# Attention outputs turned by VectorE and DMA, other step counts in the layer chain, and rectified pieces moved in the projections

## The chip, the core and the metric

The kernel runs on one core of a Trainium2 chip. The metric is device time in microseconds (us), the median of the runs shown. A core has five engines with queues of their own: TensorE (PE, matrix products into PSUM), VectorE (DVE), ScalarE (ACT), GpSimd (POOL), and SyncE (SP), which here only issues DMAs.[...]

## What is computed

Four images of 256 channels and 64 x 64 pixels go through four layers, each on a group-normed input and with its result added to the image:

```
_gn(v):    group norm, 32 groups, no affine part
layer 0:   xs = relu(group_norm(conv3x3(x)));  g, theta, phi = three 1x1 convolutions of xs to 128 channels
           y = softmax(theta^T phi) g            (4096 x 4096 for each image)
           group_norm(conv1x1(y, w_w)) * 0.1 + xs
layer 1:   rms norm, q, k, v in 4 heads of 32; linear attention (q softmax over the head, k over the pixels);
           1x1 convolution, rms norm
layer 2:   depthwise 3x3 and pointwise kernels generated from the pooled image, applied to it
layer 3:   1x1 convolution with a mix of 4 experts, weights from the pooled image
x = x + layer_i(_gn(x))     for i = 0, 1, 2, 3
```

Everything is float32. The sizes that count below: N = 4096 pixels, P = 128 partitions, NH = 2 halves of the 256 channels.

## The kernel before

**Stages.** The non-local attention of layer 0 holds most of the work. Image b's attention (`attend`) runs beside what other images need at that time: the rest of image b - 1 (`tail`: the end of layer 0 in `nonlocal_out`, then `linear_attention`, `generated`, `mixed`) and the convolution of image b + 1 (`convolve`). So there is a first convolution and projection, then stages b = 0, 1, 2, each an attention and after it the projection of the next image (`project`), then stage 3 with the attention of the last image, and an end in which that image's tail is alone. Stage 0 has only the convolution of image 1 beside it; stages 1 and 2 have a tail and a convolution; stage 3 has the tail of image 2.

**Attention.** One image has NQ = 8 blocks q of 512 queries and NM = 16 steps m of 256 keys for each. A step computes `logits` (two products of phi and theta to two banks `pf`, exponentials on ACT to `pr`) one step ahead, then the products of the probabilities with g into `py`. A block is either "across" (queries on the partitions: the row sums come out as a 129th column, L1218) or not (L1221, sums added up on DVE in `tot`). Across are q = 7 of all images and, in images 1 and 2, q in TURNED = (0, 1, 3, 5, 6).

An across block is finished by `ended`. It is a generator: its first part runs in the block's last step and normalises `py` to `yn` (query rows). Then, a step of the next block for each `yield`: `yn` is turned by four PE transposes to `ps_yt` and copied by ACT to `yt` (L1183, L1188); `yt` is multiplied by `ww_s` and copied to `wt` (L1193, L1197); `projected` takes statistics of `wt` on DVE (L1122) and stores it to `wy_d`.

**The chain.** The other layers are generators, too. They yield numbers n, in units of an attention step, or None. `Chain.steps` adds n times the stage's rate to a credit, and yields one step for each whole unit; after every step `run` issues one attention step. None is one step always, and adds rate - 1 to the credit. In `convolve` of images 2 and 3 the yields are 0, and the DVE time of what is issued is owed as time / 4.35 us, without the rate. `w.later(k, f)` calls f after k steps. If the chain still has steps when the attention has none left, they are issued back to back, with only the last parts of `ended` (q = 7) between. `while next(attention, False)` then issues what is left of the attention's steps, and `run(project(), attention)` the projection, chunk by chunk, with one more attention call after each.

**Around the changed lines.** In `linear_attention`, the tail of images 0 to 2 turns each chunk of 512 pixels by DVE's 32 x 32 block transpose (`corners`), stores to DRAM that move the blocks (`sent`), and a load (`fetched`, into quarters of `ra` and `rt`); `lengths` (L1405, ACT) is the first reader. The result `z` goes the same way at the layer's end (`z_corners`, `z_sent`, `z_fetched`), and `z_added` (L1697) adds it to the image with statistics. `generated` then starts with the group norm, whose first PE instruction is `pm` (L413). At the end of `convolve`, `normed_relu` norms the result, and `piece` applies the relu to 1024 columns of a half (four activations, L805; one, L810, for image 0) and adds it to `xs_d` by DMA. Two of the eight pieces are issued in the chain; the other six wait in `relus`, and `project` issues one for each of its first six chunks of 512 columns. A chunk is four products for phi and theta (L1029) with two ACT copies (L1030), and eight for g (L1034) with a DVE addition (L1036).

Loads and stores go through SP's queue: filters for the convolution (L587), the stores and loads named above, results. The tag k2 has four buffers of 2 KB in each partition: `yn`, `yt`, and small tiles of the layers.

Of the kernel before, what the change touches and what calls it, by code (L numbers as in the profile page):

```python
# [8 lines left out]
F32 = mybir.dt.float32  # L9
# [95 lines left out]
def conv_preact_fast(ctx: ExitStack, tc: tile.TileContext, guard, in_range, x, wc, wtpg, ww, wqkv, wout, w1cat, wd2,  # L105
# [19 lines left out]
    def k2(name):  # L125
        return wk.tile([P, 512], F32, tag="k2", name=name, bufs=4)
# [893 lines left out]
    def project(first=False):  # L1020

        if first:
            nc.gpsimd.memset(g[:, :, P:P + 1], 1.0)
        for c in range(N // 512):
            cols = bass.ts(c, 512)
            for k in (1, 0):
                ps = bank("ps_tp")
                for h in range(NH):
                    nc.tensor.matmul(ps, wtpg_s[:, h, k, :], big[:, h, cols], start=(h == 0), stop=(h == NH - 1))  # L1029
                nc.scalar.activation(tpg[:, k, cols], ps, AF.Identity, bias=btp_s[:, k:k + 1])  # L1030
            ps = bank("ps_g").rearrange("p (j o) -> p j o", o=P)
            for j in range(4):
                for h in range(NH):
                    nc.tensor.matmul(ps[:, j, :], big[:, h, bass.ts(4 * c + j, P)], wtpg_s[:, h, 2, :],  # L1034
                                     start=(h == 0), stop=(h == NH - 1))
            tt(g[:, bass.ts(c, 4), 0:P], ps, bg_s.unsqueeze(1).to_broadcast([P, 4, P]), ALU.add)  # L1036
            if relus:
                relus.pop(0)()
            yield

    NM = N // CH * 4
# [1 line left out]
    wy_stats = {}  # L1043
    sum_d = tc.dram_tile([B * NQ, P, 512], F32, name="sum_d")
    rec_d = tc.dram_tile([B * NQ, 512], F32, name="rec_d")


    res_st = cp.tile([P, NH, NQ, 6], F32, name="res_st")
# [23 lines left out]
    def attend(b):  # L1072
# [93 lines left out]
        def ended(q, py, xc):  # L1166

            at = b * NQ + q
            total, r = (sp.tile([P, 4], F32, name=name) for name in ("total", "r_q"))
            for i in range(2):  # L1170
                nc.vector.tensor_copy(total[:, bass.ts(i, 2)], py[i][:, :, P])
            nc.vector.reciprocal(r, total)
            yn = k2("yn")
            tt(yn[:, 0:2 * P].rearrange("p (t o) -> p t o", o=P), py[0][:, :, 0:P],
               r[:, 0:2].unsqueeze(2).to_broadcast([P, 2, P]), ALU.mult)
            for t in range(2, 4):
                nc.scalar.activation(yn[:, bass.ts(t, P)], py[1][:, t - 2, 0:P], AF.Copy, scale=r[:, t:t + 1])
            for side, t in enumerate((total, r)):
                nc.vector.tensor_reduce(guard[:, side, at:at + 1], t, AX.X, ALU.add)
            yield  # L1180
            pt, yt = bank("ps_yt"), k2("yt")
            for t in range(4):
                nc.tensor.transpose(pt[:, bass.ts(t, P)], yn[:, bass.ts(t, P)], ident)  # L1183
            if at == B * NQ - 1:
                nc.vector.tensor_copy(yt[:, 0:2 * P], pt[:, 0:2 * P])
                nc.scalar.copy(yt[:, 2 * P:4 * P], pt[:, 2 * P:4 * P])
            else:
                nc.scalar.copy(yt, pt)  # L1188
            yield
            wt = k4("wt").rearrange("p (h n) -> p h n", h=NH)  # L1190
            for h in range(NH):
                ps = bank("ps_wy")
                nc.tensor.matmul(ps, ww_s[:, bass.ts(h, P)], yt, start=True, stop=True)  # L1193
                if at == B * NQ - 1 and h == 0:
                    nc.vector.tensor_copy(wt[:, h, :], ps)
                else:
                    nc.scalar.copy(wt[:, h, :], ps)  # L1197
            yield
            projected(q, wt, xc)
# [156 lines left out]
    def linear_attention(w, b, big, qT, k4, st, sh, sums):  # L1356
# [129 lines left out]
        if alone:  # L1486
            w.fill(1)
            warm(3)
            w.settle()
            xg, first = normed(0), ()  # L1490
            rinv, banks = turned(xg)
            first = [product(xg, j) for j in range(2)]
            next(sums)
            xt = tokens(rinv, banks)
            yield 1
            last = None
            for c in range(NC):
                if c + 1 < NC:
                    ahead = normed(c + 1)
                next(sums, None)  # L1500
                if c == 2:
                    checks.append(counted())
                if c in (2, 4, 5):
                    next(checks[0])
                yield 0.5
                this = (yield from qk_of(xg, rinv, first)), xt
                first = ()
                if c + 1 < NC:
                    xg = ahead
                    rinv, banks = turned(xg)  # L1510
                if last is not None:
                    context(c - 1, *last)
                if c + 1 < NC:
                    xt = tokens(rinv, banks)
                last = this
            yield 1
            context(NC - 1, *last)
        else:
            w.settle()
            nc.gpsimd.memset(quarters[3].rearrange("p (k o) -> p k o", k=16)[:, :, NH * 32:TW // 4], 1.0)  # L1520
            xgs = {0: normed(0)}
            s = corners(xgs[0])
            yield 0.5
            sent(0, s)
            xgs[1] = normed(1)
            s = corners(xgs[1])
            yield 0.5
            xs = {0: fetched(0)}
            sent(1, s)
            yield 1  # L1530
            rinv = lengths(xs[0])
            last, turn = None, None
            for c in range(NC):
                if c + 1 < NC:
                    xs[c + 1] = fetched(c + 1)
                if c + 2 < NC:
                    xgs[c + 2] = normed(c + 2)
                    s = corners(xgs[c + 2])
                unit(xs[c], rinv)
                yield 0.5  # L1540
                if c + 2 < NC:
                    sent(c + 2, s)
                if c % 2 == 0:
                    if c > 0:
                        q_sent(c // 2 - 1, turn)
                    turn = k4("q_turn")
                elif c > 1:
                    q_fetched(c // 2 - 1)
                qk = yield from qk_of(xgs.pop(c), rinv)
                q_corners(c, qk, turn)  # L1550
                if last is not None:
                    context(c - 1, *last)
                if c + 1 < NC:
                    rinv = lengths(xs[c + 1])
                last = qk, xs.pop(c)
            yield 0.3
            q_sent(NC // 2 - 1, turn)
            yield 0.7
            q_fetched(NC // 2 - 1)
            context(NC - 1, *last)  # L1560
# [157 lines left out]
        yield 0.7  # L1718
        zts[NC - 1] = z_fetched(NC - 1)
        z_added(NC - 2, zts.pop(NC - 2))  # L1720
        yield 1.6
        z_added(NC - 1, zts.pop(NC - 1))
        if b + 2 < B:
            nc.gpsimd.memset(ra[:, :, :, 0:1], 0.0)
# [547 lines left out]
    def run(*steps):  # L2272

        for _ in steps[0]:
            for s in steps[1:]:
                next(s, None)
# [12 lines left out]
    with tc.manual_schedule(engines={E.PE, E.Activation, E.DVE, E.Pool, E.SP}):  # L2289
        run(Chain(convolve_first).steps())  # L2290
        run(project(first=True))
        for b in range(B - 1):
            attention = attend(b)
            parts = [tail(b - 1, big, qT), lambda w: convolve(w, b + 1, 0.53)] if b > 0 else [
                scale_weights, filters_across, lambda w: convolve(w, 1, 0.87)]
            if b == 0:
                load_x(1)
            run(Chain(both(*parts), 1.365 if b == 0 else 0.785).steps(), attention)
            while next(attention, False):
                pass  # L2300
            run(project(), attention)

        held = []
        spare = [t.rearrange("p h y x -> p h (y x)")[:, h, 0:CH] for t in (ra, rt) for h in range(NH)]
        diag = tpg[:, NH, 0:9 * P].rearrange("p (k q) -> p k q", k=9), tpg[:, NH, :]
        attention = attend(B - 1)
        run(Chain(tail(B - 2, big, qT, held=held), 1.14).steps(), attention)
        end = Chain(tail(B - 1, tpg[:, 0:NH, :], tpg[:, NH, :], in_turns(spare, k4), diag, x_cols), held=held)
        last = end.steps()
        while next(attention, False):  # L2310
            pass
        next(last)
        for part, _ in enumerate(attention):
            if part == 0:
                residual_centred()
                warm(2)
            else:
                end.fill(1)
        run(last)
        assert not held and not end.unsettled  # L2320
# [572 lines left out]
```

## Time and profile before

| what | us |
|---|---|
| median of 3 runs (lowest, highest) | 2955.13 (2953.87, 2955.23) |
| the profiled execution | 2954.07 |
| its span, first to last instruction | 2952.2 |
| attention of stage 1: first logits to last product | 743.8 to 1402.6 |
| attention of stage 2 | 1456.5 to 2116.0 |
| attention of stage 3 starts | some 2170 |

The largest groups of PE, each product counted as two passes:

| line | operation | busy us |
|---|---|---|
| L1105 | logits, 128 x 512, x2048 | 972.4 |
| L1221 | products with g, not across, x1152 | 543.5 |
| L1218 | products with g, across, x3584 | 436.8 |
| L706 | convolution, x864 | 195.8 |
| L1029 | projections of phi and theta, x256 | 117.7 |
| L1193 | products with `ww_s`, across, x56 | 29.9 |
| L1183 | transposes of `yn`, x56 | 8.6 |

The mean granted clock of PE is 0.996. A line of the order of time gives start, duration, engine, line, operation, out<-in, shape and count, and in brackets the idle time of the engine just before it with the instruction that ended it. Matmuls overlap, so the pitch of successive starts tells more than the duration. A line of windows gives, for each engine, busy time and instructions in that stretch.

### The profile page before, as it was taken

The numbers are of one execution on the slowest core, as the hardware profiler recorded it, in microseconds if no ns is written. First come the engines' busy times: TensorE is split into PE (matmuls) and PEld (weight loads), VectorE is DVE, ScalarE is ACT, GpSimd is POOL, SyncE is SP. The second block draws the span as 40 slices with busy tenths as digits, with TensorE's granted clock in tenths as the row PEclk, the third lists the DMA queues.
The fourth block names the chain that finished last, engine by engine and source line by source line (L and its number), as shares of the span: only waits on it lengthen the run. The fifth ranks groups of instructions, "written<-read, shape, count | busy, mean of one in ns | idle before, by whom it ended". The sixth has DMA issues, their size and how long they took to land. (4 is left out here: it accounts for less than half of the span.)

```text
span 2952.2 us, 31046 instructions
## 1 busy us (share of the span) xinstructions
PE 2878.1 (97%) x11158; PEld 1730.1 (59%) x11158; DVE 1851.7 (63%) x2939; ACT 1345.7 (46%) x2720; POOL 182.8 (6%) x218
## 2 busy tenths in 40 slices
PE   7999999999999999999999999999999999999999
PEld 3454555556675555777577464577655544446744
DVE  8737767752446874776254696577446578873585
ACT  2234333345556544324565543422555554433774
POOL 0000000001011000000101000000000110000143
PEclk9999999999999999999999999999999999999999
DMA  6245444324444423110554342421245563235112
GB/s 229 73 88 121 69 62 75 47 33 104 127 135 139 82 86 75 54 59 31 133 155 122 97 75 86 91 67 50 70 120 123 111 125 54 25 43 132 44 68 77
DMA packets 420642, 262.70 MB, mean 89 GB/s; under 512 B 310464, under 2 KB 357312, under 8 KB 416960
## 3 DMA queue, kind: packets, MB, share of 16 engines
q1 hardware_dynamic: 120672, 239.14, 25.1%
q10 hardware_dynamic: 295200, 4.72, 8.3%
q0 software_dynamic: 4608, 16.78, 3.6%
q8 instruction: 90, 1.47, 0.2%
q14 instruction: 72, 0.59, 0.1%
HBM read 162.84 MB, written 114.53 MB: 94 GB/s over the span
## 5 line engine op out<-in xcount | busy, mean ns | idle before, releaser
L1106 ACT ACTIVATE pr<-pf 128x512 f32<-128x512 f32 x1024 | 600.4, 596 | 912.1 <-PE pf L1105 871.0
L1105 PE MATMUL pf<-tpg 128*128 128x512 f32 x2048 | 972.4, 598 | 2.4 <-ACT pr L1106 2.4
L1105 PEld LDWEIGHTS pf<-tpg 128*128 128x128 f32 x2048 | 378.4, 191 | 372.4 <-issue 348.7
L1221 PE MATMUL py<-pr,tpg 128*128 128x512 f32 x1152 | 543.5, 594 | 0.3 <-ACT pr L1106 0.3
L1218 PEld LDWEIGHTS py<-tpg,pr 128*128 128x128 f32 x3584 | 434.7, 192 | 109.5 <-issue 100.3
L1218 PE MATMUL py<-tpg,pr 128*128 128x129 f32 x3584 | 436.8, 275 | 2.6 <-ACT pr L1106 2.6
L138 DVE TENSOR_TENSOR tot<-tot,pr 128x1024 f32<-128x1024 f32 x252 | 307.5, 1220 | 165.2 <-ACT pr L1106 164.4
L1221 PEld LDWEIGHTS py<-pr,tpg 128*128 128x128 f32 x1152 | 220.3, 191 | 278.7 <-issue 269.2
L141 DVE SCALAR_TENSOR_TENSOR dw<-xp,dk,dw 128x1008 f32<-128x1008 f32 x192 | 243.1, 1270 | 7.3 <-ACT dw L1866 3.6
L706 PE MATMUL ps_conv<-v,u 128*128 128x256 f32 x864 | 195.8, 380 | 1.3 <-DVE v L138 1.1
L706 PEld LDWEIGHTS ps_conv<-v,u 128*128 128x128 f32 x864 | 161.8, 190 | 31.3 <-issue 8.8
L233 POOL TENSOR_TENSOR rstd<-rstd,half 128x2 f32<-128x2 f32 x24 | 17.7, 736 | 1941.5 <-DVE rstd L431 1795.6
L1029 PE MATMUL ps_tp<-big,wtpg_s 128*128 128x512 f32 x256 | 117.7, 597 | 6.0 <-ACT big L805 5.3
L1455 PE MATMUL ps_qk<-wqkv_s,xg 128*128 128x256 f32 x496 | 115.0, 382 | 7.1 <-ACT pr L1106 7.1
L138 DVE TENSOR_TENSOR tpg<-ps_g,bg_s 128x512 f32<-128x512 f32 x32 | 22.1, 692 | 154.5 <-PE ps_g L1034 154.5
L141 DVE SCALAR_TENSOR_TENSOR sums<-ps_conv,sums 128x512 f32<-128x512 f32 x72 | 49.7, 691 | 94.6 <-PE ps_conv L706 86.4
L1455 PEld LDWEIGHTS ps_qk<-wqkv_s,xg 128*128 128x128 f32 x496 | 93.7, 191 | 24.5 <-ACT pr L1106 7.9
L1874 PE MATMUL ps_pw<-dw,pk 128*128 128x512 f32 x192 | 86.3, 593 | 0.0
L1029 PEld LDWEIGHTS ps_tp<-big,wtpg_s 128*128 128x128 f32 x256 | 46.0, 192 | 57.5 <-issue 42.7
L1030 ACT ACTIVATE tpg<-ps_tp,btp_s 128x512 f32<-128x512 f32 x64 | 44.0, 687 | 71.7 <-PE ps_tp L1029 71.7
L1122 DVE BATCH_NORM_STATS2 wy_st<-wt 128x6 f32<-128x512 f32 x64 | 42.8, 688 | 47.8 <-ACT wt L1159 33.7
L2196 ACT ACTIVATE res<-ps_ex,b 128x512 f32<-128x512 f32 x56 | 38.2, 686 | 72.6 <-PE ps_ex L2188 69.4
(486 smaller groups left out, 3256.8 us busy)
## 6 DMA issues: line engine op xcount, KB each, us to landing
u<-filters SPq DMA_DIRECT2D x72, 256.0 KB, 2.6
xp<-in_x_dram SPq DMA_DIRECT2D x16, 1024.0 KB, 7.6
xs_d<-big POOLq DMA_DIRECT2D x32, 512.0 KB, 6.1
wy_d<-wt SPq DMA_DIRECT2D x32, 512.0 KB, 3.0
wy<-wy_d SPq DMA_DIRECT2D x32, 512.0 KB, 5.6
out_dram<-res SPq DMA_DIRECT2D x64, 256.0 KB, 2.0
turned_d<-rt SPq DMA_DIRECT2D x96, 130.0 KB, 2.5
xs_d<-in_x_dram SPq DMA_DIRECT2D x24, 512.0 KB, 6.7
```

The source lines that it names most:

```text
L138: nc.vector.tensor_tensor(o, a, b, op)
L141: nc.vector.scalar_tensor_tensor(o, a, s, b, op0, op1)
L706: nc.tensor.matmul(ps[:, bass.ts(oh, IY * IX)], u[i][:, h, bass.ts(oh, P)], v[:, i, bass.ts(h, IY * IX)], start=(h == 0), stop=(h == NH - 1))
L1029: nc.tensor.matmul(ps, wtpg_s[:, h, k, :], big[:, h, cols], start=(h == 0), stop=(h == NH - 1))
L1030: nc.scalar.activation(tpg[:, k, cols], ps, AF.Identity, bias=btp_s[:, k:k + 1])
L1105: nc.tensor.matmul(pf, phi[:, bass.ts(2 * m + s, P)], theta[:, bass.ts(q, 512)], start=True, stop=True)
L1106: nc.scalar.activation(pr[:, bass.ts(s, 512)], pf, AF.Exp)
L1122: nc.vector.bn_stats(st[:, h, q, :], wt[:, h, :])
L1218: nc.tensor.matmul(py[t // 2][:, t % 2, :], probs[i][:, s * 512 + t * P:s * 512 + (t + 1) * P], g[:, 2 * m + s, :], start=(begin and t % 2 ...
L1221: nc.tensor.matmul(py, g[:, 2 * m + s, 0:P], probs[i][:, bass.ts(s, 512)], start=begin, stop=end)
L1455: nc.tensor.matmul(ps[:, 0:2 * HID], xg[:, h, bass.ts(j, P)], wqkv_s[:, h, 0:2 * HID], start=(h == 0), stop=(h == NH - 1))
L1874: nc.tensor.matmul(ps, pk[:, h * NH * P + oh * P:h * NH * P + (oh + 1) * P], dw[h][:, bass.ts(s, 512)], start=(h == 0), stop=(h == NH - 1))
```

## The change

It has four parts. In `project`, the rectified piece is issued ahead of a chunk's products and copies and no longer after them. In `ended`, across blocks other than q = 7 are turned in another way: a DVE block transpose of `yn` to `y_turn`, four stores to a new DRAM tile `y_d` that move the blocks, one load to `yt`, then the products with `ww_s`; the columns come out in another order, and ACT's copy to `wt` puts them right. These parts lie over seven steps of the next block in place of three. In `linear_attention`, the chain yields one unit more between the first fetch and `lengths` (1 to 2), and one more ahead of the last `z_added` (1.6 to 2.6). The rate of stages 1 and 2 goes from 0.785 to 0.82.

```diff
--- before.py
+++ after.py
@@ -1023,6 +1023,8 @@
             nc.gpsimd.memset(g[:, :, P:P + 1], 1.0)
         for c in range(N // 512):
             cols = bass.ts(c, 512)
+            if relus:
+                relus.pop(0)()
             for k in (1, 0):
                 ps = bank("ps_tp")
                 for h in range(NH):
@@ -1034,8 +1036,6 @@
                     nc.tensor.matmul(ps[:, j, :], big[:, h, bass.ts(4 * c + j, P)], wtpg_s[:, h, 2, :],
                                      start=(h == 0), stop=(h == NH - 1))
             tt(g[:, bass.ts(c, 4), 0:P], ps, bg_s.unsqueeze(1).to_broadcast([P, 4, P]), ALU.add)
-            if relus:
-                relus.pop(0)()
             yield
 
     NM = N // CH * 4
@@ -1043,6 +1043,7 @@
     wy_stats = {}
     sum_d = tc.dram_tile([B * NQ, P, 512], F32, name="sum_d")
     rec_d = tc.dram_tile([B * NQ, 512], F32, name="rec_d")
+    y_d = tc.dram_tile([NQ, 4, 32, 4, P], F32, name="y_d")
 
 
     res_st = cp.tile([P, NH, NQ, 6], F32, name="res_st")
@@ -1177,6 +1178,29 @@
                 nc.scalar.activation(yn[:, bass.ts(t, P)], py[1][:, t - 2, 0:P], AF.Copy, scale=r[:, t:t + 1])
             for side, t in enumerate((total, r)):
                 nc.vector.tensor_reduce(guard[:, side, at:at + 1], t, AX.X, ALU.add)
+            if q < NQ - 1:
+                yield
+                s = k2("y_turn")
+                nc.vector.transpose(s.rearrange("p (a t e) -> p a t e", a=4, t=4), yn.rearrange("p (t a r) -> p a t r", t=4, a=4))
+                yield
+                for k in range(4):
+                    nc.sync.dma_start(out=y_d[q, :, :, k, :].rearrange("a r n -> r a n"),
+                                      in_=s[bass.ts(k, 32), :].rearrange("p (a n) -> p a n", a=4))
+                yield
+                yield
+                yt = k2("yt")
+                nc.sync.dma_start(out=yt, in_=y_d[q].rearrange("a r c n -> (a r) (c n)"))
+                yield
+                yield
+                wt = k4("wt").rearrange("p (h n) -> p h n", h=NH)
+                for h in range(NH):
+                    ps = bank("ps_wy")
+                    nc.tensor.matmul(ps, ww_s[:, bass.ts(h, P)], yt, start=True, stop=True)
+                    nc.scalar.copy(wt[:, h, :].rearrange("p (t c e) -> p c t e", t=4, c=4),
+                                   ps.rearrange("p (c t e) -> p c t e", c=4, t=4))
+                yield
+                projected(q, wt, xc)
+                return
             yield
             pt, yt = bank("ps_yt"), k2("yt")
             for t in range(4):
@@ -1527,7 +1551,7 @@
             yield 0.5
             xs = {0: fetched(0)}
             sent(1, s)
-            yield 1
+            yield 2
             rinv = lengths(xs[0])
             last, turn = None, None
             for c in range(NC):
@@ -1718,7 +1742,7 @@
         yield 0.7
         zts[NC - 1] = z_fetched(NC - 1)
         z_added(NC - 2, zts.pop(NC - 2))
-        yield 1.6
+        yield 2.6
         z_added(NC - 1, zts.pop(NC - 1))
         if b + 2 < B:
             nc.gpsimd.memset(ra[:, :, :, 0:1], 0.0)
@@ -2295,7 +2319,7 @@
                 scale_weights, filters_across, lambda w: convolve(w, 1, 0.87)]
             if b == 0:
                 load_x(1)
-            run(Chain(both(*parts), 1.365 if b == 0 else 0.785).steps(), attention)
+            run(Chain(both(*parts), 1.365 if b == 0 else 0.82).steps(), attention)
             while next(attention, False):
                 pass
             run(project(), attention)
```

## The prediction

> **What bounds it now.** I read the page's first two parts, then the list of who waited for whom on TensorE (PE), then PE in order of time around each wait. The page says that PE is the bound:
>
> ```profile
> PE 2878.1 (97%) x11158; PEld 1730.1 (59%) x11158; DVE 1851.7 (63%) x2939; ACT 1345.7 (46%) x2720; POOL 182.8 (6%) x218
> ```
>
> Its idle time is 2952.2 - 2878.1 = 74 us, so a change can pay in two ways only: less PE work, or smaller holes. VectorE (DVE) and ScalarE (ACT) matter where they make a hole. In order of time, the holes that this change can touch are of four kinds. Columns: start, duration, engine, line, operation, and in brackets the idle time before it and what ended it.
>
> ```profile
> 1422.38 1.02 PE L1029 MATMUL ps_tp<-big,wtpg_s 128*128 128x512 f32 x2
> 1424.08 2.84 PE L1029 MATMUL ps_tp<-big,wtpg_s 128*128 128x512 f32 x6 [0.68 <-ACT big L805]
> ...
> 1516.23 2.45 PE L1455 MATMUL ps_qk<-wqkv_s,xg 128*128 128x256 f32 x8 [3.65 <-ACT pr L1106]
> 1518.47 3.16 PE L1105 MATMUL pf<-tpg 128*128 128x512 f32 x4
> ...
> 1656.90 0.39 PE L413 MATMUL pm<-mv,avg 128*128 128x2 f32 x2 [4.36 <-DVE mv L138]
> 1657.14 3.36 PE L1105 MATMUL pf<-tpg 128*128 128x512 f32 x4
> ```
>
> (1) In a projection, PE waits for a rectified piece. (2) In linear attention, PE waits for ACT. (3) Before the group norm of layer 2, PE waits for DVE. (4) At the end of a stage, shown further down, it waits for both. Each of 2 and 3 costs more than its brackets: the four logit passes at 1518.47 and 1657.14 take 3.16 and 3.36 us, where the usual four take 1.88. The windows after the like hole at 943 show why (last columns: granted clock, DMA share, GB/s):
>
> ```profile
> 943.00:946.00 3.00, 2.90 (x6) 1.38 (x7) 2.87 (x7) 0.60 (x1) 0.00 (x0) 0.70 0.25 56
> 946.00:949.00 3.00, 3.00 (x8) 1.46 (x7) 0.12 (x2) 0.60 (x1) 0.00 (x0) 0.73 0.32 124
> ```
>
> At clocks 0.70 and 0.73 PE loses 3 x 0.30 + 3 x 0.27 = 1.7 us. [...] the hole at 2248 was 2.41 us, and the windows after it have 0.51 and 0.92, again 1.7 us. [...] The holes of 0.7 us leave the clock at 1.00.
>
> **Pieces ahead of the chunk.** The holes of kind 1 after the first projection are 0.66 and 0.67 (b = 0 to 1), 0.68, 0.66, 0.67, and three of 0.66: 5.3 us. A chunk takes PE 5.2 us, the four activations of a piece 2.6 us; emitted one chunk's evictions earlier, each piece ends before the chunk that reads it. **-5.3**. The first projection's 0.65 waits for the second piece, which isn't moved: 0.
>
> **One more step for the first turned chunk.** What is late here is a DMA:
>
> ```profile
> 1512.85 0.42 ACT L1405 ACTIVATE junk<-ra 128x256 f32<-128x256 f32 x1 [7.10 <-DMA ra<-turned_d]
> ```
>
> ACT stands for 7.10 us in front of `lengths`, with the next exponentials queued behind it; PE runs dry after one step. The PE holes are 3.49, 3.65 and 2.41 us in the three stages that have it, 9.55 in all, and three slow clocks add 5.1. A step is 3.5 us of PE work (logits 1.72, products with g 1.78). Adding up the layers' yields with their credits, stages 1 and 2 go from one step to two between the fetch and `lengths`, with one more ahead of the fetch; stage 3 also gains one. That covers the holes: **-14.7**.
>
> **One more step for the last.** Holes 3.92 and 4.36 (stage 3 has none), clocks 2 x 1.7. Between the last `z_sent` and the `pm` product there are four steps now and five after, 3.4 us more; the two statistics of `wt` (1.28 us on DVE, in front of `mv`) come later too, because the output of q = 1 is now ready later. Together 4.7 us, which closes both: **-11.7**.
>
> **Turning by DVE and DMA.** Ten blocks (q = 0, 1, 3, 5, 6 of b = 1 and 2) lose four PE transposes. Successive starts give 0.43 us for four (703.25 to 703.68): **-4.3**. [...] the trace's pitch is 0.107, so 4.3. The block moves are the DMAs. ACT loses ten copies of 585 ns, which were hidden. DVE gains ten transposes, with this row nearest:
>
> ```profile
> L1416 DVE STREAM_TRANSPOSE q_turn<-qk x24: 710/711/714, 806.7 to 2313.6; 128x512 f32<-128x512 f32 x24
> ```
>
> That is 7.1 us, beside PE at 63% busy DVE: 0; uncovered, 7.1. The reordering copies of `wt` have no row; between L1197 (0.585 us) and the 1.9 times by which a reordering relu (810 ns for 256 columns, against 418 in order) exceeds its like: 0 to 11 us of ACT over 20 copies, hidden at 46%: 0. On SP each block adds four stores (1.75 us, landing 2.3 as `z_d`) and a fetch (0.34, landing 3.5): 8 us after the store step. Five steps of the attention, 17 us, lie between yn and the product with ww, four after the stores. A fetch waits for the stores' landing, and behind it stand other loads of SP, the filters (L587) above all, which are asked for a product ahead. Bounds: nothing, or a late `yt`, behind which all of PE is queued, at 2.8 us of wait and 1.7 of clock for a block. I take 0. Three 2 KB buffers per block rather than two of the four add no wait that I can find: only `pk` or `w2` is alive beside them.
>
> **The denser rate.** This is the loss. Stages 1 and 2 have 128 attention steps. Their layers have 29 bare hops, 91.90 units and 34.02 units owed by the convolution (not scaled by the rate): 0.785 x (29 + 91.90) + 34.02 = 128.9, 130 steps since the last hops run into debt. So they end two steps past the attention already. Kind 4, end of stage 1:
>
> ```profile
> 1400.62 0.28 PE L413 MATMUL pm<-mv,avg 128*128 128x2 f32 x2
> 1400.76 2.03 PE L1218 MATMUL py<-tpg,pr 128*128 128x129 f32 x16
> 1402.63 0.28 PE L429 MATMUL pv<-ev,avg 128*128 128x2 f32 x2
> 1403.72 0.66 PE L1183 MATMUL ps_yt<-ident,yn 128*128 128x128 f32 x4 [0.81 <-DVE yn L138]
> 1408.49 3.62 PE L1193 MATMUL ps_wy<-yt,ww_s 128*128 128x512 f32 x4 [4.11 <-ACT yt L1188]
> 1411.94 3.60 PE L1029 MATMUL ps_tp<-big,wtpg_s 128*128 128x512 f32 x8
> ```
>
> From the end of the last attention product (1402.6) to the projection it takes 9.3 us. After, 28 hops and 93.90 units at 0.82 and the same debt to the convolution give 133.9: 134 steps. The convolution's last product then falls one step before the attention's last, and all that follows it on DVE is bare:
>
> ```profile
> 1374.37 2.50 DVE L141 SCALAR_TENSOR_TENSOR rt<-sums 128x512 f32<-128x512 f32 x4
> 1378.08 0.69 DVE L141 SCALAR_TENSOR_TENSOR rt<-ps_conv,rt 128x512 f32<-128x512 f32 x1 [1.21 <-PE ps_conv L706]
> 1379.80 0.69 DVE L141 SCALAR_TENSOR_TENSOR rt<-ps_conv,rt 128x512 f32<-128x512 f32 x1 [1.03 <-PE ps_conv L706]
> 1380.53 2.36 DVE L138 TENSOR_TENSOR xp<-xp,rt 128x1024 f32<-128x1024 f32 x2
> 1382.81 2.46 DVE L688 BATCH_NORM_STATS2 st<-xp 128x6 f32<-128x512 f32 x4
> 1385.19 0.38 DVE L370 BATCH_NORM_AGGREGATE mv<-st 128x2 f32<-128x24 f32 x2
> ```
>
> In DVE's order from 1402.6 on: yn 1.1, these 2.5 + 1.4 + 2.4 + 2.5 + 0.4, the moments 1.75 (1390.70 to 1392.45), `pm` to `ev` 1.1 with the statistics of `wt` 1.3 between, `pv`, power and affine 1.9, then two pieces on ACT at 2.44: 21.1 us, plus 1.7 for a cold clock at the projection. That is 22.8 - 9.3 = 13.5 for a stage: **+27.0**. Stage 3 goes from 122 to 125 steps of 128: 0.
>
> **Sum.** -5.3 - 14.7 - 11.7 - 4.3 + 27.0 = -9.0; five closed holes may leave 0.3 each, as waits of 0.2 to 1.0 stand elsewhere (+1.5): -7.5. The profiled execution took 2954.07, so 2946.6; the median of the runs shown is 1.06 above it: **2947.6 us**.
>
> **Rivals.**
> - A, slower: the stage ends cost more. One more step in the layers moves 3.5 us of cover away, in each of two stages. With two more steps (hops that come and go with the convolution's pace) 14 us are added: 2962. It decides above 17 us for a stage in place of 13.5; that PE has nothing else there speaks for it, that the yields add up exactly for the kernel before against.
> - B, slower: late `yt` on SP. Waits of SP on filters reach 30.4 us; if the four blocks of q = 5 and 6 wait at 4.5 us each, 2966. It decides from 1.9 us a block. Against it: four steps of lead.
> - C, faster: DVE runs ahead at the stage's end and the tail is 7 us shorter in both: 2934.
> - D: the holes of kinds 2 and 3 only move, since their DMA round trips are as long as before and another consumer stands at their end; half of 26.4 stays: 2961, with the rest kept.
>
> **Chances.** Forecast 0.50, own range 2942 to 2953; A 0.18, B 0.10, C 0.12, D 0.10. No change is within 5.9 us (0.2%) of 2955.1, about what a measurement can tell. Faster: 0.36 of the forecast, 0.12 of C, 0.04 of the rest: 0.52. Slower: the larger parts of A and B and a little of D: 0.20. Same: 0.28. Range 2938 to 2962.
>
> **What would show it.** No waits above 1 us at L1455, L1105 and L413 in mid-stage and clock 1.00 there; no wait for L805 within a projection; no PE transpose in mid-stage and no wait for `yt` there; at both stage ends some 21 us from the last attention product to the first projection, with the join, the row joins and the statistics after it on DVE. I am wrong if those ends cost below 7 or above 17 us each, or if new waits for `yt` or `v` appear.

## The result, and the profile after

The change made the kernel slower: 2962.17 us (2959.92 to 2965.53, 12 runs) against 2955.19 (2953.87 to 2958.18, 12 runs) for the kernel before, a ratio of 1.0024 with an interval of 1.0015 to 1.0032. That is +7.0 us where -7.5 was forecast. The profiled span went from 2952.2 to 2961.6 us.

The page's first part says little of it: PE is busy 1.8 us less than before, and idle for 85.3 us where it was 74.1 (span less busy time). Slow clock is hidden in the busy time: the mean granted clock fell from 0.996 to 0.992.

```profile
PE 2876.3 (97%) x11118; PEld 1727.6 (58%) x11118; DVE 1854.6 (63%) x2949; ACT 1335.3 (45%) x2710; POOL 184.7 (6%) x218
```

The waits that the change was to close did close. These lines of PE in order of time answer to those shown of before: no bracket stands behind the second chunk's `ps_qk` of linear attention in stages 1 and 2 (3.49 and 3.65 there), none behind `pm` in mid-stage (3.92 and 4.36), and inside the projections no wait of 0.66 for L805 is left.

```profile
804.98 3.62 PE L1479 MATMUL ps_qk<-wqkv_s,xg 128*128 128x256 f32 x16
...
944.86 0.28 PE L413 MATMUL pm<-mv,avg 128*128 128x2 f32 x2
...
1524.41 3.62 PE L1479 MATMUL ps_qk<-wqkv_s,xg 128*128 128x256 f32 x16
```

The end of stage 1 got longer, as predicted. From the last attention product (1398.5) to the second chunk of the projection (1425.23) it takes 26.7 us, where it took 14.4; in stage 2 it is 25.6, where it also took 14.4. (To the first chunk it is 18.3, where it was 9.2 and some 21 was forecast; the first chunk's first eight products then take another 6.6 us where they took 3.4; the granted clock is 0.50 until 1422.44.) PE stands for `yn`, `yt`, the moments, the variance (1.34 at 1411.80), and the first rectified piece, one after another. For the last the profile names no releaser; ACT works on the pieces from 1414.08:

```profile
1396.58 1.95 PE L1242 MATMUL py<-tpg,pr 128*128 128x129 f32 x16
1399.54 0.63 PE L1207 MATMUL ps_yt<-ident,yn 128*128 128x128 f32 x4 [1.01 <-DVE yn L138]
1401.71 3.57 PE L1217 MATMUL ps_wy<-yt,ww_s 128*128 128x512 f32 x4 [1.54 <-ACT yt L1212]
1409.87 0.59 PE L413 MATMUL pm<-mv,avg 128*128 128x2 f32 x2 [4.58 <-DVE mv L138]
...
1416.80 2.05 PE L1031 MATMUL ps_tp<-big,wtpg_s 128*128 128x512 f32 x2 [4.45 <-issue]
```

What was not predicted is in the list of who waited for whom (total, times, longest). `v` and `dw` were no entries of this size before, and `yt` by DMA is new:

```profile
PE ps_conv L706 <- DVE v L138: 7.9, 4, 2.9
PE ps_pw L1898 <- DVE dw L141: 6.0, 2, 3.0
...
PE ps_wy L1198 <- DMA yt<-y_d: 3.5, 2, 2.1
```

In order of time these are 1.40 (`yt`), 3.01 (`dw`), 1.07 and 2.86 (`v`) in stage 1, and 2.06, 3.01, 1.07 and 2.86 in stage 2. With two waits of 0.69 and 0.37 for `pr` that is 18.4 us (the two of 1.07 stand where the kernel before had 0.52 and 0.56, so 17.3 are new). Behind three of them the clock is slow, at 0.50: for 3.41 us behind each of those for `dw` (from 1070.87 and 1791.09), and for 6.83 us behind the longer one for `v` in stage 2 (from 1961.75). The window from 1071 has a granted clock of 0.50, the one behind `v` is shown in the last section:

```profile
1071.00:1074.00 3.00, 2.69 (x3) 1.18 (x4) 3.00 (x4) 0.00 (x0) 0.00 (x0) 0.50 0.00 0
```

The cause of `dw` stands on DVE 18 us earlier. This is VectorE in order of time, from the end of turned block q = 3 of stage 1:

```profile
1043.92 2.57 DVE L141 SCALAR_TENSOR_TENSOR dw<-xp,dk,dw 128x1008 f32<-128x1008 f32 x2
1053.30 0.16 DVE L1172 COPY total<-py 128x2 f32<-128x2 f32 x1 [6.81 <-PE py L1242]
...
1055.84 3.76 DVE L141 SCALAR_TENSOR_TENSOR dw<-xp,dk,dw 128x1024 f32<-128x1024 f32 x3
1059.52 0.70 DVE L1184 STREAM_TRANSPOSE y_turn<-yn 128x512 f32<-128x512 f32 x1
1060.15 3.85 DVE L141 SCALAR_TENSOR_TENSOR dw<-xp,dk,dw 128x1024 f32<-128x1024 f32 x3
```

`ended` begins in the block's last step with a copy of the row sums out of `py`, and these are there only when PE has made the block's last product. DVE comes to the copy early, stands 6.81 us, and the depthwise taps that it could have computed meanwhile are queued behind (m1, below, shows that it could). It has given up its lead; the `y_turn` of 0.70 us comes on top, and PE stands for `dw` at 1071. The same happens at 1229, where DVE stands 7.33 us and `v` is late at 1243. Over the whole kernel DVE stands at this copy 67.2 us, where it was 44.4 before.

### The profile page after: what moved, and what is told of

Same layout as the page of the kernel before. It is cut to its first block, busy times and chain, and to the rows that moved or that the text cites. A ratio compares the mean times of both kernels' runs of the same rounds, so it can differ in the third digit from the quotient of the medians.

```text
span 2961.6 us, 31082 instructions
## 1 busy us (share of the span) xinstructions
PE 2876.3 (97%) x11118; PEld 1727.6 (58%) x11118; DVE 1854.6 (63%) x2949; ACT 1335.3 (45%) x2710; POOL 184.7 (6%) x218
## 5 line engine op out<-in xcount | busy, mean ns | idle before, releaser
L706 PE MATMUL ps_conv<-v,u 128*128 128x256 f32 x864 | 198.7, 384 | 7.9 <-DVE v L138 7.9
L706 PEld LDWEIGHTS ps_conv<-v,u 128*128 128x128 f32 x864 | 163.5, 193 | 38.2 <-DVE v L138 8.9
L138 DVE TENSOR_TENSOR tpg<-ps_g,bg_s 128x512 f32<-128x512 f32 x32 | 22.1, 691 | 161.5 <-PE ps_g L1036 161.5
L805 ACT ACTIVATE big<-xp,sh,sc 128x256 f32<-128x256 f32 x96 | 62.6, 814 | 20.9 <-DVE sh L138 20.9
L1036 PEld LDWEIGHTS ps_g<-wtpg_s,big 128*128 128x128 f32 x512 | 62.2, 192 | 15.3 <-issue 15.3
```

The costliest lines, as they stand in the source:

```text
L138: nc.vector.tensor_tensor(o, a, b, op)
L706: nc.tensor.matmul(ps[:, bass.ts(oh, IY * IX)], u[i][:, h, bass.ts(oh, P)], v[:, i, bass.ts(h, IY * IX)], start=(h == 0), stop=(h == NH - 1))
L805: nc.scalar.activation(image[:, h, tiles, k, :].rearrange("p i (t j) -> p i j t", j=MX), outs[:, h, k].rearrange("p j (i t) -> p i j t", t ...
```

## The experiments

Differences below are medians against the kernel before in the same set of runs, with the interval of the ratio turned into us. That kernel's median was 2955.6 in the first set, 2958.1, 2957.8 and 2957.6 in the others. The kernel after was timed only with the result, so a difference between it and a run below is a difference of two rows. "Copy" is the time that DVE stands at the copy of row sums; "ends" is the time from the last attention product to the second chunk, stages 1 and 2. "L706" is a wait ahead of a convolution product for which the profile names no releaser.

| run | difference, us | copy | ends | waits of PE above 1.5 us in mid-stage 1 |
|---|---|---|---|---|
| before | 0 | 44.4 | 14.4, 14.4 | pr 3.49, mv 3.92 |
| after | +7.0 | 67.2 | 26.7, 25.6 | dw 3.01, v 2.86 |
| e1_rate_back | -13.3 (-17.1 to -9.2) | 37.2 | 15.2, 15.1 | pr 4.39, v 3.21 |
| e2_turn_only | -0.4 (-3.0 to +1.8) | 44.4 | 14.2, 14.4 | pr 3.42, mv 5.30 |
| e3_relu_steps | -8.0 (-12.1 to -5.3) | 37.2 | 14.6, 14.7 | pr 3.21, v 3.22 |
| e4_rate_only | +5.2 (+3.8 to +7.7) | 48.8 | 20.6, 20.5 | mv 4.33, L706 2.09 |
| m1_defer | -12.7 (-16.3 to -8.3) | 22.1 | 27.1, 26.1 | none |
| m2_no_turn | -2.8 (-5.0 to -0.3) | 67.9 | 26.4, 26.7 | mv 1.61, dw 1.56 |
| m3_no_steps | +2.1 (0.0 to +4.1) | 48.8 | 20.0, 20.3 | mv 6.77, dw 1.64, L706 2.52 |
| m4_rate_76 | -26.4 (-29.9 to -21.9) | 39.0 | 15.2, 14.9 | none |
| n1_lead | +5.7 (+3.0 to +7.7) | 67.2 | 27.1, 26.8 | dw 3.00, v 2.86 |
| n2_two_turns | +11.7 (+7.4 to +15.4) | 67.2 | 27.3, 27.3 | yt 1.73, dw 3.75, v 3.61 |
| n3_defer_76 | -28.0 (-32.2 to -23.4) | 10.6 | 15.7, 15.2 | none |
| n4_rate_74 | -25.3 (-29.3 to -21.3) | 69.5 | 5.5, 5.5 | mv 4.59, dw 1.62, v 1.82 |
| n5_defer_74 | -28.3 (-31.6 to -22.8) | 42.6 | 5.5, 5.5 | mv 4.78, v 1.86 |
| p1_before_74 | -10.3 (-14.8 to -6.8) | 61.1 | 5.5, 5.5 | pr 3.48, yn 2.59, v 2.40 |
| p2_before_later | -5.7 (-8.0 to -3.8) | 11.8 | 14.5, 14.6 | pr 3.59, mv 1.87, yn 1.87 |
| p3_pieces | -6.2 (-8.3 to -3.8) | 44.4 | 14.5, 15.8 | pr 3.64, mv 5.27 |

### The parts of the change

The kernel after with the old rate:

```diff
-            run(Chain(both(*parts), 1.365 if b == 0 else 0.82).steps(), attention)
+            run(Chain(both(*parts), 1.365 if b == 0 else 0.785).steps(), attention)
```

> The changed kernel with the rate of stages 1 and 2 back at 0.785; pieces, step counts and turning stay. The layers then take 130 steps in place of 134. Theory 1 (the later layers do the harm: bare stage ends, some 12 us each against the kernel before, and new mid-stage waits of PE on dw and v, some 9 us for a stage, because a block's end on DVE now falls just ahead of work that PE needs): both stage ends are as before, at some 9 us from the last attention product to the projection, the waits at L1898 and L706 go back to under 1 us, and the time is 2920 to 2935. Theory 2 (the turning on DVE and by DMA makes the mid-stage waits): the stage ends come back, the waits on dw and v stay, 2937 to 2942. Theory 3 (the rate is harmless): 2962.

The kernel before with the turning alone (the other three parts left as they were):

```diff
+    y_d = tc.dram_tile([NQ, 4, 32, 4, P], F32, name="y_d")
...
+            if q < NQ - 1:
+                yield
+                s = k2("y_turn")
...
+                return
```

> The kernel before with the turning of attention outputs alone. Theory 1: 4.3 us of transposes saved on PE, nothing else moved, at most 3.5 us of waits for yt: 2951 to 2955. Theory 2: new waits of 3 us at ps_pw and ps_conv with a slow clock behind each, 2965 to 2972.

The kernel before with the pieces ahead of the chunk and both step counts:

```diff
+            if relus:
+                relus.pop(0)()
             for k in (1, 0):
...
-            yield 1
+            yield 2
...
-        yield 1.6
+        yield 2.6
```

> The kernel before with the pieces ahead of the chunk and the two step counts, without the turning and at rate 0.785. Theory 1: 5.3 us of waits for pieces, 14.7 for the first turned chunk and 11.7 for the last are gone, the stage ends stay (130 steps): 2923 to 2931. Theory 2 says the same. If the holes only move (rival D of the prediction): 2937 or more.

The kernel before with the new rate alone:

```diff
-            run(Chain(both(*parts), 1.365 if b == 0 else 0.785).steps(), attention)
+            run(Chain(both(*parts), 1.365 if b == 0 else 0.82).steps(), attention)
```

> The kernel before with the rate of stages 1 and 2 at 0.82 alone: 133 steps in place of 130. Theory 1: the stage ends cost some 9 to 12 us more each and the mid-stage waits on dw and v appear without any turning, 2972 to 2995. Theory 2: only the stage ends cost more, 2972 to 2979, and no wait of 2 us or more at ps_pw and ps_conv. Theory 3: 2955.

No part has a price of its own. From 0.785 to 0.82 costs 5.2 us alone, but 20.3 on top of all the rest (after less e1). The turning is worth -0.4 alone and -5.3 beside pieces and steps at 0.785 (e1 less e3, whose intervals overlap). And the step counts, forecast at -26.4, bring little: e3 is at -8.0, of which the pieces alone (p3, below) are -6.2, and those intervals overlap too. In e3 the old holes are closed, but PE then stands 3.21 us for `pr` and 3.22 for `v`. Of the four forecasts of time, two came near: e2 (2955.2) lies at the edge of its first theory, and e3 (2947.6) is where the holes that only move were expected. e1 (2942.3) missed its first theory by 7 us and lies at the edge of the second, whose wait for `dw` did not stay. e4 (2960.8) fits none of its three.

The rate alone (e4) makes neither of the waits that were seen after, so the first theory, which laid them on the rate, fell in part. But it makes one of the same kind at another block, in both stages. DVE stands 7.93 us at the copy, the joins of `xp` and the first part of `v` are queued behind it, and PE starts its convolution when that part is done, at 1326.99:

```profile
1320.66 0.16 DVE L1171 COPY total<-py 128x2 f32<-128x2 f32 x1 [7.93 <-PE py L1218]
...
1327.09 3.69 PE L706 MATMUL ps_conv<-v,u 128*128 128x256 f32 x16 [2.09 <-issue]
```

The `v` of e3 shows another face of the same thing. These are lines of VectorE in order of time: the end of a block that is not turned puts its reduction (L1142, 1.11 us, with two small instructions 1.4) just between the norm and the taps that PE needs, and PE starts on `v` at 1197.15, 3.22 us late. Before, the reduction stood behind the first part of `v` and the wait was 0.52. Another 1.0 of the difference is a wait of PE for `pr` that stood just ahead before and is gone here, so that PE comes sooner.

```profile
1180.99 7.60 DVE L766 TENSOR_SCALAR big<-xp,gm,rstd 128x1024 f32<-128x1024 f32 x6
1188.48 1.11 DVE L1142 TENSOR_REDUCE r_inv<-inv 128x4 f32<-128x512 f32 x1
```

Its `pr` is late because ACT, too, stands at a block's end: at 921.61 it had waited 3.39 us for `r_q` (the inverse row sums) with work for linear attention and the next exponentials queued behind, and at 925.87 another 1.75 us for POOL.

### One step later, and the parts taken out again

The kernel after, with the first part of a turned block's end one step later:

```diff
+            if q < NQ - 1:
+                yield
             at = b * NQ + q
```

> The kernel after, with the first part of a turned block's end (its copy of the row sums, the normalising and all that follows) one attention step later. Phase theory: DVE stands at that copy until PE has made the block's last product, gives up its lead there, and PE then waits for dw and v; a step later the product is already made, so DVE's waits at that copy fall from 67 us to below 35, the waits for dw (3.0 us) and v (1.1 and 2.9) fall below 1 us in both stages, and the time is 2945 to 2952. Rival, the amount of DVE work (ten more transposes and denser layers) makes the waits: they stay, within 3 us of 2962.

The kernel after without the turning:

```diff
-            if q < NQ - 1:
-                yield
-                s = k2("y_turn")
...
-                return
```

> The kernel after without the turning by VectorE and DMA. Phase theory: the rate with the step counts puts the block ends where they hurt, so waits for dw and v of 2 us and more stay in mid-stage, those for yt are gone there, and the transposes cost 4 us: 2958 to 2963. Rival, the turning's own DVE work and DMAs make the mid-stage waits: none above 1 us is left, 2943 to 2949.

The kernel after without the two step counts:

```diff
-            yield 2
+            yield 1
...
-        yield 2.6
+        yield 1.6
```

> The kernel after without the two step counts. Phase theory: the layers stand to the block ends as in the kernel before at the same rate, whose waits for dw and v were 0.7 us; that kernel's 2960.8 less 5.3 for the pieces and up to 4.3 for the transposes: 2951 to 2956. Rival, the turning makes the waits: dw and v at 2 us and more stay, 2960 to 2967.

The kernel after at a lower rate:

```diff
-            run(Chain(both(*parts), 1.365 if b == 0 else 0.82).steps(), attention)
+            run(Chain(both(*parts), 1.365 if b == 0 else 0.765).steps(), attention)
```

> The kernel after at a rate of 0.765. By the credits the layers of stages 1 and 2 then end after 126 steps of the attention's 128 in place of 134, so nothing of them is left for the stage's end: from the last attention product to the projection it takes below 8 us in both stages (26.9 after, 14.5 before). If no new mid-stage wait opens: 2932 to 2939. Rival, the place of the layers against the block ends decides as much as the end: waits of 3 us and more for other consumers appear in mid-stage, and the time is 2942 or more.

m1 tells most. It takes away no work and no DMA, and its ends are as long as after; it is 19.7 us faster (-12.7 against +7.0). VectorE of m1 in order of time, at the same block end:

```profile
1047.66 0.69 DVE L1912 SCALAR_TENSOR_TENSOR big<-ps_pw,big 128x512 f32<-128x512 f32 x1 [2.04 <-PE ps_pw L1900]
...
1049.99 3.76 DVE L141 SCALAR_TENSOR_TENSOR dw<-xp,dk,dw 128x1024 f32<-128x1024 f32 x3
1053.67 0.22 DVE L1174 COPY total<-py 128x2 f32<-128x2 f32 x2
```

The two additions of `ps_pw` and three taps, which came after the copy, now run in the time in which DVE stood; the copy, issued a step later, finds its products made, and no bracket stands behind it. The waits for `dw` are gone, of those for `v` the longer ones are gone and 1.05 and 1.03 are left (below 1 was expected), and those for `yt` are gone as well. Expected were 2945 to 2952; 2945.4 came. The run moves all of the block's end, ACT's part of it too; the copy alone was not moved.

m2 splits the rest. Without the turning DVE stands at the copy just as long (67.9), so the rate with the step counts places the block ends there. But `dw` is then late by 1.56 and 1.44 rather than 3.01 once, and `v` by 1.03: the turning makes the lost lead dearer, 9.8 us (+7.0 less -2.8, with its waits for `yt` in it), though it takes 40 transposes off PE. Expected were 2958 to 2963 by the one theory and 2943 to 2949 by the other; 2955.3 came, between them, so both hold a part.

m3 missed its 2951 to 2956 with 2960.2. The rival's 2960 to 2967 has the number, but not the rival's waits: `dw` is at 1.64. Without its step, the hole for `mv` grew to 6.77 us (3.92 before, 4.33 with the rate alone). `mv` is not later: it is ready at 941.01, where with the rate alone it was ready at 942.77, and DVE's wait of 2.51 us for the last load of `z` was 2.54 in the kernel before. But PE comes sooner, at 934.30 in place of 938.50. Half of that are the transposes and the products with `ww_s` of block q = 1, 2.15 us by successive starts: they stood ahead of `pm` with the rate alone; turned the new way, the block has no such transposes, and its products come behind `pm` (947.76). The other half I have not followed.

m4 was expected to gain at the stage's end and did not: its ends take 15.2 and 14.9 us, as in e1, since the layers still reached into the attention's last step (`pv` at 1392.94, the last product at 1393.08). My count of 126 steps was wrong: 0.765 x (28 + 93.90) + 34.02 is 127.3. It gained in mid-stage, where e1's waits of 4.39 for `pr` and 3.21 for `v` are gone. The 2931.7 us lie at the edge of the expected 2932 to 2939, for another reason than the one given: luck. DVE still stands 7.33 us at a copy there (1238.68), and no wait of PE above 0.6 us follows in mid-stage. A lead lost at the copy costs only what is due soon after it.

### What is the DMA's, what is DVE's, and lower rates

One more step between the load of `yt` and its products; each transpose twice; both of the last section's gains together; a still lower rate (all on the kernel after):

```diff
+                yield
                 wt = k4("wt").rearrange("p (h n) -> p h n", h=NH)
```

> The kernel after, with one more attention step between the load of yt and the products that read it. It parts the turning's DMAs from its DVE work. Theory: of the turning's cost only the waits for yt (1.40 and 2.06) are its DMAs' doing; they fall below 0.4, the waits for dw (3.0) and v (2.9) stay, and the time falls by 3 to 5: 2957 to 2960. Rival, the statistics of wt, now a step later still, get in front of the moments that pm waits for: a wait for mv of 2 us or more opens in both stages, 2962 to 2970.

```diff
                 nc.vector.transpose(s.rearrange("p (a t e) -> p a t e", a=4, t=4), yn.rearrange("p (t a r) -> p a t r", t=4, a=4))
+                nc.vector.transpose(s.rearrange("p (a t e) -> p a t e", a=4, t=4), yn.rearrange("p (t a r) -> p a t r", t=4, a=4))
```

> The kernel after with each DVE transpose to y_turn done twice (the output is the same): ten more of 0.70 us. Theory: where DVE has lost its lead at a block's end, each 0.7 us queued on it shows on PE: dw goes from 3.0 to some 3.7, v from 2.9 to some 3.6 and from 1.1 to 1.8, in both stages, with no other new wait: 2965 to 2970. Rival, the transposes hide in DVE's idle time, and the turning's cost lies in its DMAs and copies: 2961 to 2964.

```diff
+            if q < NQ - 1:
+                yield
             at = b * NQ + q
...
-            run(Chain(both(*parts), 1.365 if b == 0 else 0.82).steps(), attention)
+            run(Chain(both(*parts), 1.365 if b == 0 else 0.765).steps(), attention)
```

> The kernel after at a rate of 0.765 and with the first part of a turned block's end one step later, both together. At 0.765 alone there was no wait for dw or v above 0.6 to take away, so theory: the one-step delay has nothing to gain, 2929 to 2934. Rival, the waits of 0.9 to 1.5 for pr, qk and z there come from the same copy of row sums: they go too, 2922 to 2928.

```diff
-            run(Chain(both(*parts), 1.365 if b == 0 else 0.82).steps(), attention)
+            run(Chain(both(*parts), 1.365 if b == 0 else 0.74).steps(), attention)
```

> The kernel after at a rate of 0.74. By the credits its layers end after 124 of the 128 steps. Theory: the stage's end is already as short as the last block lets it be at 126 steps, so nothing more is won there (within 1 us of it), and what decides is where the layers fall against the block ends: between 2931 and 2950, with waits of 2 us or more in mid-stage if above 2938. Rival, fewer steps always pay, through the end: below 2929.

n1 took the waits for `yt` away and gained next to nothing: +5.7 against +7.0, within the intervals, since waits for `mv` of 0.70 and 0.95 came and one for `dw` of 0.92. Its 2963.4 missed the expected 2957 to 2960. The wait itself is one of SP's queue. In its order of time after the change, the fetch of `yt` for q = 1 stands behind stores and a load of `z`, 6.2 us after its own stores had been issued:

```profile
927.38 1.91 SPq L1187 DMA_DIRECT2D y_d<-y_turn  x4
...
931.24 1.84 SPq L1709 DMA_DIRECT2D z_d<-rt  x4
935.03 0.34 SPq L1714 DMA_DIRECT2D ra<-z_d  x1
935.48 0.36 SPq L1192 DMA_DIRECT2D yt<-y_d  x1
```

n2 shows the price of DVE work behind a lost lead: `dw` went from 3.01 to 3.75 and the longer `v` from 2.86 to 3.61, in both stages, by 0.74 and 0.75 for a transpose of 0.71. The shorter `v` didn't move (1.07 to 1.04). The time rose by 4.7 us over after (+11.7 against +7.0).

n3, expected to gain nothing over m4 or 4 us and more, gained 1.6 (-28.0 against -26.4), inside both intervals. The waits of 0.7 to 1.5 for `qk`, `pr` and `z` stayed: they don't come from the copy, whose waits fell from 39.0 to 10.6.

n4's 2932.4 lies in the expected 2931 to 2950, but not as expected: its ends fell to 5.5 us, where I had expected none of that. PE in order of time shows why. Nothing of the layers is left, and the last block's end lies between the projection's chunks:

```profile
1399.06 3.73 PE L1242 MATMUL py<-tpg,pr 128*128 128x129 f32 x32
1402.63 3.60 PE L1031 MATMUL ps_tp<-big,wtpg_s 128*128 128x512 f32 x8
...
1407.85 0.60 PE L1207 MATMUL ps_yt<-ident,yn 128*128 128x128 f32 x4
```

9.7 and 9.4 us were won there against m4, and all of it given back in mid-stage: `mv` 4.59 and 5.53, `dw` 1.62, `v` 1.82.

### The same causes in the kernel before

The kernel after at 0.74 with the end one step later; and the kernel before with one edit each (the edits have been shown): the rate 0.74, the end one step later, the pieces.

```diff
+            if q < NQ - 1:
+                yield
             at = b * NQ + q
...
-            run(Chain(both(*parts), 1.365 if b == 0 else 0.82).steps(), attention)
+            run(Chain(both(*parts), 1.365 if b == 0 else 0.74).steps(), attention)
```

> The kernel after at a rate of 0.74, with the first part of a turned block's end one step later. At 0.74 alone DVE stood 69.5 us at that copy and PE waited for dw (1.6) and v (1.8) in both stages, and for mv 4.6 and 5.5, where DVE itself stood 2.48 for a load of z. Lost lead makes the waits for dw and v, the round trip through DRAM the one for mv: the copy's waits fall below 40 us, dw and v below 0.6, mv stays at 3 or more, 25 to 31 below the kernel before less another 4 to 7: 29 to 33 us below it. Rival: lost lead makes all three, 38 us or more below it.

> The kernel before with a rate of 0.74 alone. The stages' ends (14.4 us from the last attention product to the second chunk) should fall to some 5.5 as they did in the kernel after at that rate, 17.8 in both. Theory: the rate is the lever, and the change's other parts add their own: 14 to 20 us below the kernel before, with the waits for mv of 3.9 and 4.4 kept. Rival: without the step counts the denser mid-stage gives as much back in waits for pr, mv, dw or v: within 6 us of it.

> The kernel before with the first part of a turned block's end one step later, alone. DVE stood 44 us at the copy of row sums there. Theory: lost lead costs only where a producer's result is due within the steps behind it, and the kernel before has no waits for dw or v: within 4 us of the kernel before, though the copy's waits fall below 25 us. Rival: every us of DVE's waiting at the copy costs in part: 8 us or more below it.

> The kernel before with the rectified pieces moved ahead of the chunk, alone. The prediction's first term by itself: eight waits of 0.66 go, 5.3 us below the kernel before, no other wait. Rival: the wait moves to the first chunk, whose copies then stand behind the piece on ACT: within 2 us of it.

n5 is at -28.3, as fast as n3 and a little short of what was expected, with 42.6 us at the copy where less than 40 was. The wait for `dw` went, that for `mv` stayed as expected (4.78), where DVE itself stands 2.03 us for the load of `z`; but `v` stayed at 1.86. There DVE works without a break from the norm (1164.76) to the first part of `v` (1177.49), with no copy between, so that wait is not lost lead, as I had said, but that chain's own length. p1 came between its two theories, -10.3: 8.9 us were won at each end, and 2.59 for `yn` and 2.40 for `v` came up in mid-stage. p2 came between as well, -5.7. DVE's waits at the copy fell to 11.8, and the wait for `mv` from 3.92 to 1.87. But that is not lost lead: at the copy of this block (q = 1, 923.30) DVE did not stand in the kernel before. The hole was split: PE stands 1.87 us for the later `yn` first, and the statistics of `wt` (1.28 us) fall behind `mv` in place of ahead of it. In the kernel before, 3.41 us at a clock of 0.50 followed the hole (from 944.18); p2's clock there is not shown. So why p2 gains is in part open; the two traces differ by 2.1 us only. p3 is -6.2, and -5.3 is inside its interval.

## Why the prediction was wrong

- **Pieces ahead of the chunk, -5.3**: right. The eight waits went, and p3 measured -6.2 (-8.3 to -3.8). In its trace the wait for `mv` is longer than before (5.27 for 3.92), so not every part of it agrees.
- **Step counts, -14.7 and -11.7**: the holes closed in the kernel after, as worked out. But in the kernel before, with the pieces, they brought some 2 us (e3 less p3, not clear of the noise) and not 26.4. The rival "the holes only move" described this, with a chance of 0.10, and put half of it back; nearly all came back.
- **Transposes, -4.3**: -5.3 beside pieces and steps at the old rate, but -0.4 in the kernel before and +9.8 in the change as a whole. The ten DVE transposes take 702 ns each, 711 were taken.
- **The denser rate, +27.0**: mechanism right, 23.5 measured (12.3 and 11.2, where 13.5 each was forecast; the summands there make 21.2 and 134.0, not 21.1 and 133.9, which changes nothing). The order of DVE's work behind the last product is the one predicted. What was missing is that a rate also moves everything in mid-stage: alone it lengthened each end by some 6.2 us, yet cost only 5.2 in all. The step counts lengthen the ends by as much again (20.0 and 20.3 without them, m3), so the 23.5 are not the rate's alone.
- **What the closed holes leave, +1.5**: this is the step that failed, with "That is 7.1 us, beside PE at 63% busy DVE: 0" beside it. New waits of 18.4 us came, with three slow stretches of the clock that by an estimate cost another 6.8 (13.65 us at 0.50), and m1 shows what they are: with the block's end one step later the same work costs 19.7 us less. I looked at each consumer that waited before and asked if it would be on time; I did not ask which producers would fall behind a copy that itself waits for PE, once steps, rate and block ends stood differently to each other. The average of 63% says nothing of that, since DVE stood idle at the copy while work was queued behind it.
- **Late `yt` (rival B)**: it was late, at q = 1 behind `z` and not at q = 5 and 6 behind filters, and at 3.5 us in all. n1 shows that closing it moves the time by little.
- **Rival A** (the ends cost more) is out: they cost less than forecast.

With 18.4 for 1.5, and 23.5 for 27.0, the sum is +5.9 in place of -9.0 + 1.5, and +12.7 with the 6.8 of the slow clocks. The two profiled executions differ by 9.4 us and the medians by 7.0, so the sum does not close by 3 to 6 us. That the failed term carries the miss is shown by m1; how much of it each wait carries is not, as most runs that removed one wait opened another.

## What to carry to other kernels

Look for instructions that wait for the bottleneck engine (here a copy of row sums at a block's end, at which VectorE stood 67.2 us in the kernel after), and list what is queued behind them: issuing such an instruction a step later took no work away here and gave 19.7 us in the kernel after, but 1.6 at a rate of 0.765 (n3 less m4), where nothing due soon stood behind it. When a wait is closed by moving work, size the next producer's slack before counting the gain, since closing a hole makes every later deadline earlier. Where two chains of fixed steps run beside each other, a rate is a phase as well as a speed: it is measured, over several values, after every other change; here 0.765 and 0.74 with the end one step later gave 2929.8 and 2929.3 us, faster than both kernels.

## What was unexpected of the hardware

Equal holes of PE did not do equal things to its clock. The wait of 2.86 us for `v` in stage 2 was followed by a window at 0.50 (the last line below); that of 2.86 us in stage 1 was followed by 1.00 throughout. What differs is their place. In the traces of the kernels before and after, all changes of the clock, by its own record there, lie whole multiples of 3.413 us apart (within 3 ns). Cut into windows at these multiples, the hole in stage 1 falls into two, and PE is busy for 2.15 and 1.81 us of them; in stage 2 it is busy for 1.33 of one:

```profile
1238.13:1241.54 3.41, 2.15 (x17) 1.75 (x15) 3.38 (x4) 0.74 (x2) 0.00 (x0) 1.00 0.53 151
1241.54:1244.95 3.41, 1.81 (x8) 1.63 (x9) 3.34 (x5) 0.00 (x0) 0.00 (x0) 1.00 0.01 3
1244.95:1248.37 3.42, 3.42 (x13) 2.28 (x12) 3.36 (x6) 1.19 (x2) 0.00 (x0) 1.00 0.38 116
1958.34:1961.75 3.41, 1.33 (x12) 1.14 (x11) 3.38 (x4) 0.18 (x1) 0.00 (x0) 1.00 0.44 128
1961.75:1965.17 3.42, 2.63 (x6) 2.16 (x7) 3.28 (x6) 0.00 (x0) 0.00 (x0) 0.50 0.00 0
```

Counted so over each of the two traces, from the first record of the clock on (some 23 us), every window at full clock in which PE stood for more than 2.00 us was followed by one at 0.50 (8 of 8 before, 7 of 7 after), and none with 1.64 us or less was. Of the three between, one was: 1.68 us after, at 132.21, but not 1.68 before, at 131.81, nor 1.96 after, at 2955.03. The hole of 2.41 us at 2248 in the kernel before lies in one window (2244.66 to 2248.07).

The slow stretches of mid-stage after lasted 3.41, 3.41 and 6.83 us, whole multiples of 3.41. The 6.83 us came behind a window in which PE stood for 2.08 us only (stage 2, above). Why the clock falls, and why the windows between 1.64 and 2.00 us differ, these traces do not show.
